# Layer 1 of a two-layer graph network: logits as eight 64-column products, and another order of ScalarE's work at a group's end

## The chip, the cores and the metric

The kernel runs on one core of a Trainium2 chip. Such a core has TensorE (PE in the profile; PEld are its weight loads), VectorE (DVE), ScalarE (ACT), GpSimd (POOL) and SyncE (SP, which here only starts DMAs). They run side by side and wait for one another through semaphores. TensorE writes its products into PSUM, eight banks of 512 f32 columns on 128 partitions[...]. The metric is the device time of one execution in microseconds (us).

## The reference

Two layers work on x (4096 x 512) and a weighted adjacency matrix adj (4096 x 4096). Layer 0 is a dense attention with adj added to its logits. The change is in layer 1, a graph attention with 8 heads of 64 columns:

```python
nX = (x @ W).reshape(n, NHEAD, OUT_DIM).transpose(1, 0, 2)      # then each head's rows are standardized
at1 = jnp.einsum('kno,ok->kn', nX, a1)[:, :, None]
at2 = jnp.einsum('kno,ok->kn', nX, a2)[:, :, None]
kg = jax.nn.leaky_relu(at1 + at2.transpose(0, 2, 1), negative_slope=LK_ALPHA)
kg = kg * graph[None, :, :]
mg = jnp.where(mask[None, :, :], kg, NEG_FILL)
attention = jax.nn.softmax(mg, axis=-1)
y = attention @ nX + nX
...
return jax.nn.elu(y)
```

graph and mask are adj and its nonzero places. So for each head there is a 4096 x 4096 matrix of logits, each the leaky relu of a sum of two numbers, times the edge's weight, with absent edges pushed far down; then an exponential, and a product with the head's values.

## The kernel before, in words

Layer 0 takes a little over the first half of the span and is not touched. Layer 1 then runs 512 steps (STEPS in `fast_path`): 8 chunks of 512 targets (ic) x 2 groups of 4 heads (hg) x 32 blocks of 128 sources (jt). One step handles 128 sources x 512 targets for 4 heads: sources lie on the partitions, targets along the 512 columns. The 32 steps of one (ic, hg) are a group; its results gather in `accs`, a PSUM tile of two banks.

The order of the work is written out by hand: `seq` keeps each engine's instructions in the order of the program text, and the framework puts the semaphores in. The loop at the end of `fast_path` issues for step n:

- `sums(n)`, on TensorE. `z_product` (L1065) makes the sum of the two numbers of each head as a product with only 6 rows to sum over: bf16 pieces of the one number against ones, and ones against pieces of the other. Head number hh sits on partitions 32 hh to 32 hh + 5, so that the four heads use different rows of TensorE's array and run side by side. Two heads (hh 1 and 3) start in the banks r0 and r1; the other two (hh 0 and 2) are added onto what already stands in the tile `l` (two banks). Then eight products with 64 x 64 parts of an identity (L1095) add the masks, in two waves of four that run side by side.
- `left_sums(n + 1)` (L1075), on TensorE: four products of 64 rows and 64 columns, the first part of the next step's `l`; ScalarE turns it by `left_relu` (L1081). The relu has to be done before the next step's `z_product` of hh 0 and 2.
- `right_leaky(n)` (L1113), on VectorE, from r0 and r1 into the SBUF tile `t` (six buffers); `right_weigh(n)` (L1119) on GpSimd multiplies by the edges' weights; `left_weigh(n)` (L1122) on VectorE does that for the heads in `l`.
- `values(n - 4, 0)` and `values(n - 4, 1)` (L1134), on TensorE: f32 products of 64 columns, two heads side by side, added in `accs`.
- `exponent(n - 2)` (L1126), on ScalarE, over all of `t`.

`l` has two buffers and r0 and r1 one each.

At a group's end (step n in which n - 4 was the group's last block) `finish` empties `accs`: ScalarE copies one bank (L1187) and VectorE the other (L1188). Over the next four steps, in the "mid" place between the two halves of the values, `to_rows` (L1198) turns a quarter back to rows on TensorE and `divide` (L1210, L1211) divides it on VectorE; GpSimd's DMAs, an exponential (L1237) and the store follow some steps later. In the kernel before, ScalarE's exponential of step n - 2 is done in two halves there, heads 0 and 1 ahead of its copy and heads 2 and 3 after it. For the 15 groups before the last this is so; at the last group's end no exponential is left to do.

Of the kernel before, what the change touches and what calls it, by code (L numbers as in the profile page):

```python
# [18 lines left out]
P = 128  # L19
# [3 lines left out]
HD = 64  # L23
# [56 lines left out]
def fast_path(  # L80
# [18 lines left out]
    nc = tc.nc  # L99
    seq = tc.keep_in_program_order  # L100
# [155 lines left out]
    def two_halves(t):  # L256
        return t.rearrange("p (g c) -> p g c", g=2)
# [68 lines left out]
    with tc.tile_pool(name="rows_in", bufs=2) as rows_in, tc.tile_pool(  # L326
# [70 lines left out]
        with tc.tile_pool(name="proj_v", bufs=1) as pv, tc.tile_pool(  # L397
# [209 lines left out]
            for k in range(KC):  # L607
                pa = psum.tile([P, 512], F32, name="pa", tag="XZ"[k % 2], bufs=2)
                for c in range(SB):
                    seq(nc.tensor.matmul(  # L610
                        pa, turned["q"][:, c, ts(k, P)], turned["k"][:, c, :],
                        start=c == 0, stop=c == SB - 1,
# [42 lines left out]
            for sb in range(NS):  # L655
                if sb + 2 < NS:
                    xts[sb + 2] = load_x(sb + 2)
                if sb == 1:
                    for k in range(KC):
                        seq(nc.sync.dma_start(  # L660
                            out=w1_sb[:, k, :, 0 : D // 2], in_=two_halves(w1[ts(k, P), :])
# [22 lines left out]
        with tc.tile_pool(name="turns", bufs=6) as turns, tc.tile_pool(  # L684
# [238 lines left out]
            for s in range(0, n_tiles, 2):  # L923
                ic, jt = TILES[s]
# [63 lines left out]
    with tc.tile_pool(name="ga_g", bufs=2) as adjs, tc.tile_pool(  # L988
# [5 lines left out]
        JB = 4  # L994
# [3 lines left out]
        loads, logits, groups = {}, {}, {}  # L998
# [7 lines left out]
        def load_adj(q):  # L1006
            ic, _, jt = STEPS[q * JB]
            z2 = inputs.tile([P, JB * P], BF16, name="z2", tag="z2", bufs=2)
            seq(nc.sync.dma_start(
                out=z2, in_=z2_d[:, STEPS[q * JB][1], jt * P : (jt + JB) * P]  # L1010
            ))
            ng = inputs.tile([P, JB, GC], BF16, name="nb", tag="nb", bufs=2)
            seq(nc.sync.dma_start(
                out=ng, in_=nT_d[jt : jt + JB, :, ts(ic, GC)].rearrange("t p i -> p t i")
            ))

            nx = inputs.tile([P, JB, GC], BF16, name="nx", tag="nx", bufs=2)
            for r in range(2):
                seq(nc.sync.dma_start(
                    out=nx[ts(r, HD)],  # L1020
                    in_=nT_d[jt : jt + JB, ts(1 - r, HD), ts(ic, GC)].rearrange("t p i -> p t i"),
                ))
            g = adjs.tile([P, JB, GC], F32, name="g", tag="g", bufs=2)
            seq(nc.sync.dma_start(
                out=g, in_=gT_d[jt : jt + JB, :, ts(ic, GC)].rearrange("t p i -> p t i")
            ))
            loads[q] = (g, (ng, nx), z2)
# [5 lines left out]
        def open_group(n, queue):  # L1033

            ic, hg, _ = STEPS[n]
            z1_left = z1_lefts[(2 * ic + hg) % 2]
            for first in (0, HD):
                rows = slice(first, first + 6)
                seq(queue.dma_start(out=z1_left[rows, :], in_=z1_d[rows, hg, ts(ic, GC)]))
            z1 = inputs.tile([P, GC], BF16, name="z1", tag="z1", bufs=2)  # L1040
            seq(queue.dma_start(out=z1, in_=z1_d[:, hg, ts(ic, GC)]))
            u4 = inputs.tile([P, 2, GC], F32, name="u4", tag="u4", bufs=2)
            groups[ic, hg] = {"z1": z1, "z1_left": z1_left, "u4": u4}
            load_u4(n, 0, queue)

        def load_u4(n, e, queue):
            ic, hg, _ = STEPS[n]
            seq(queue.dma_start(
                out=groups[ic, hg]["u4"][:, e, :].rearrange("p (b i) -> p b i", i=P),
                in_=u4_d[ic * SB : (ic + 1) * SB, hg * HG + 1 + 2 * e, :]  # L1050
                .unsqueeze(0).to_broadcast([P, SB, P]),
            ))
# [8 lines left out]
        def z_product(n, hh, out, start):  # L1061

            ic, hg, jt = STEPS[n]
            rows = slice(32 * hh, 32 * hh + 6)
            seq(nc.tensor.matmul(  # L1065
                out, loads[n // JB][2][rows, ts(jt % JB, P)], groups[ic, hg]["z1"][rows, :],
                start=bool(start), stop=False, skip_group_check=not start,
            ))

        def left_sums(n):  # L1070

            lefts[n] = psum.tile([P, 2, GC], F32, name="l", tag="l", bufs=2)
            ic, hg, jt = STEPS[n]
            for r, c in ((0, 0), (1, 1), (0, 1), (1, 0)):
                seq(nc.tensor.matmul(  # L1075
                    lefts[n][ts(c, HD), r, :], loads[n // JB][2][ts(r, HD), jt % JB * P + c * HD :][:, :HD],
                    groups[ic, hg]["z1_left"][ts(r, HD), :], start=True, stop=True,
                ))
# [4 lines left out]
        def sums(n):  # L1083

            jt = STEPS[n][2]
            left = lefts[n]
            right = [psum.tile([P, GC], F32, name=f"r{e}", tag=f"r{e}", bufs=1) for e in range(2)]
            out = [left[:, 0, :], right[0], left[:, 1, :], right[1]]
            for hh in (1, 3, 0, 2):
                z_product(n, hh, out[hh], hh % 2)  # L1090
            masks = loads[n // JB][1]
            for first in (1, 0):
                for r, c in ((0, 0), (1, 1), (0, 1), (1, 0)):
                    rows = ts(r, HD)
                    seq(nc.tensor.matmul(  # L1095
                        out[first + 2 * r][ts(c, HD), :], ident_b[rows, rows],
                        masks[r != c][rows, jt % JB, :], start=False, stop=True,
                        skip_group_check=first == 0,
                    ))
            rights[n] = right  # L1100
# [23 lines left out]
        def exponent(n, heads=slice(0, HG)):  # L1124
            t = logits[n][:, heads, :]
            seq(nc.scalar.activation(t, t, AF.Exp))  # L1126
# [28 lines left out]
        def check_early():  # L1155
            ends = work.tile([P, 3], F32, name="ends0", tag="ends0", bufs=1)
            seq(nc.vector.tensor_reduce(ends[:, 0:1], low0, AX.X, ALU.min))
            seq(nc.vector.tensor_reduce(ends[:, 1:2], high0, AX.X, ALU.max))
            seq(nc.vector.tensor_scalar(good[:, 0:1], ends[:, 0:1], TINY, None, ALU.is_ge))
            seq(nc.vector.tensor_scalar(good[:, 1:2], ends[:, 1:2], HUGE0, None, ALU.is_le))  # L1160
            seq(nc.vector.tensor_scalar_mul(ends[:, 2:3], ends[:, 0:1], SPREAD))
            seq(nc.vector.tensor_tensor(good[:, 2:3], ends[:, 1:2], ends[:, 2:3], ALU.is_le))
            check_inverses(3, of_all[:, : of_all.shape[1] - of_last])
# [372 lines left out]
        for n in range(n_steps + 4):  # L1536

            q = n // JB + 1
            if n == n_steps:

                check_early()
                last_in.append(work.tile([P, HG, GC], F32, name="t", tag="t", bufs=6))
                for k, ap in enumerate((own_d[NI - 1, :, :, 1], x1_d[NI - 1, 1])):
                    seq(nc.sync.dma_start(
                        out=last_in[0][:, 2 * k : 2 * k + 2, :].rearrange("p f c -> p (f c)")
                        .rearrange("p (b d) -> p b d", b=SB),
                        in_=ap.rearrange("p b f d -> p b (f d)"),
                    ))
            if n % JB == 0 and q < n_steps // JB:
                load_adj(q)  # L1550
            if n + 10 < n_steps and STEPS[n + 10][2] == 0:
                open_group(n + 10, nc.sync)
            if n + 6 < n_steps and STEPS[n + 6][2] == 0:
                load_u4(n + 6, 1, nc.sync)
            if n < n_steps:
                sums(n)
            for f in left.pop(n, []):
                f()
            if n + 1 < n_steps:
                left_sums(n + 1)  # L1560
            if n < n_steps:
                right_leaky(n)
                right_weigh(n)
            if n + 1 < n_steps:
                left_relu(n + 1)
            done, ready = 0 <= n - 4 < n_steps, 0 <= n - 2 < n_steps
            if done and n < n_steps + 1:
                values(n - 4, 0)
            extra(n, "mid")
            if n < n_steps:  # L1570
                left_weigh(n)
            if done:
                if n < n_steps + 1:
                    values(n - 4, 1)
                if n % JB == 3:
                    loads.pop((n - 4) // JB)
            if n == n_steps + 3:
                for m, hf in ((n - 6, 0), (n - 5, 0), (n - 6, 1), (n - 5, 1)):
                    values(m, hf)
                for hf in range(2):  # L1580
                    values(n - 4, hf)
            if done and STEPS[n - 4][2] == NB - 1:
                if ready:
                    exponent(n - 2, slice(0, 2))
                finish(n, *STEPS[n - 4][:2])
                if ready:
                    exponent(n - 2, slice(2, 4))
            elif ready:
                exponent(n - 2)
            extra(n, "end")  # L1590
# [404 lines left out]
```

## Time and profile before

| | |
|---|---|
| median of 3 runs | 3541.22 us (3538.57 to 3542.74) |
| the profiled execution | 3538.39 us |
| its span, first to last instruction | 3536.6 us |
| granted TensorE clock | 0.996 |
| step 0's first logits product (L1065) | 1935.3 us into the span |
| a usual step of layer 1 | 2.967 us |
| values (L1134) | 4096 matmuls, 605 ns each in the records |
| logits (L1065) | 2048 matmuls, 386 ns |
| masks (L1095) | 4096 matmuls, 402 ns into r, 378 ns into l |
| left sums (L1075) | 2048 matmuls, 380 ns |

The span is what the profile shows from the first instruction to the last; about 1.8 us of the execution lie around it. A matmul's length in a record is modelled, and products on different parts of the array overlap, so that the lengths don't add up to time: what counts is when the next kind of product starts. In a row of the profile the line, the engine and the operation come first, then what is written and read by the program's names, the shape (`6*128` is 6 rows and 128 columns of weights), the count, the busy time in us and after it the mean of one in ns, and last the idle time before it with what ended it.

### The profile page before, as it was taken

The page shows a single profiled execution, that of the slowest core. Times are in us where ns is not written, and L with a number is a line of the kernel's source. Part 1 is how long each engine was busy: PE and PEld are TensorE (multiplying, and loading weights), DVE is VectorE, ACT ScalarE, POOL GpSimd, SP SyncE. Part 2 cuts the span into 40 slices and gives each one's busy share as a digit, 9 for nine tenths or more (in the row PEclk, how much of TensorE's full clock was granted, in tenths as well). Part 3 has the DMA queues.
Part 4 walks back from the last instruction along what each step waited for, and adds up shares of the span by engine and source line. Part 5 has one row for each costly group of instructions (what it writes and reads, how often), then busy time and mean ns, then how long its engine had stood idle before and what let it go on. Part 6 is the DMA issues. An engine that isn't in the chain of part 4 may idle for free.

```text
span 3536.6 us, 59808 instructions
## 1 busy us (share of the span) xinstructions
PE 3492.0 (99%) x21898; PEld 2149.6 (61%) x21898; DVE 2574.3 (73%) x4262; ACT 1771.1 (50%) x1580; POOL 2285.6 (65%) x1863
## 2 busy tenths in 40 slices
PE   9999999999999999999999999999999999999998
PEld 7888888888888888888887223223222323232232
DVE  6765665656565666656567888888888888888887
ACT  2100111111111111111133999999999999999997
POOL 6754444444444444444567888788888888888886
PEclk9999999999999999999999999999999999999999
DMA  6688888888888888888768777787778877777885
GB/s 226 219 247 246 233 232 250 234 244 247 235 246 247 231 252 241 237 248 232 235 135 183 210 207 204 205 208 214 211 209 219 214 215 206 198 209 209 214 213 147
DMA packets 633550, 779.07 MB, mean 220 GB/s; under 512 B 78560, under 2 KB 461216, under 8 KB 624032
## 3 DMA queue, kind: packets, MB, share of 16 engines
q1 hardware_dynamic: 615680, 742.34, 73.5%
q0 software_dynamic: 16464, 31.98, 5.3%
q8 instruction: 174, 2.85, 0.3%
q10 hardware_dynamic: 1104, 0.85, 0.1%
q14 instruction: 128, 1.05, 0.1%
HBM read 592.97 MB, written 174.19 MB: 217 GB/s over the span
## 4 chain that ended last, share of the span: by engine, by line
PE 90%; DVE 7%; ACT 1%; DMA 1%; issue 1%; SPq 0%; DVEq 0%; ACTq 0%
PE accs L1134 25%; PE XZ L722 21%; PE M L777 20%; PE r L1095 4%; PE r L1065 4%; PE l L1075 3%; PE X L508 3%; PE l L1095 3%; PE Z L508 2%; DVE t L1122 2%; PE y L1327 1%; PE pt L1198 1%; DVE x L837 1%; DVE y L1211 1%; PE accs L1327 1%
## 5 line engine op out<-in xcount | busy, mean ns | idle before, releaser
L1119 POOL TENSOR_TENSOR t<-t,g 128x1024 f32<-128x1024 f32 x512 | 1225.6, 2406 | 268.9 <-DVE t L1113 233.3
L1134 PE MATMUL accs<-t,nX 128*64 128x512 f32 x4096 | 1003.0, 605 | 4.6 <-DVE ob L1188 4.6
L1126 ACT ACTIVATE t<-t 128x2048 f32<-128x2048 f32 (+1 forms) x527 | 976.5, 1853 | 0.2 <-POOL t L1119 0.2
L1113 DVE SCALAR_TENSOR_TENSOR t<-u,at2m,r 128x512 f32<-128x512 f32 x1024 | 719.3, 744 | 194.2 <-issue 152.0
L738 ACT ACTIVATE aT<-aT 128x512 f32<-128x512 f32 x256 | 161.2, 630 | 1387.3 <-DVE aT L734 1387.3
L734 DVE TENSOR_TENSOR aT<-aT,XZ 128x256 f32<-128x256 f32 x884 | 348.7, 418 | 575.1 <-PE XZ L722 570.8
L1122 DVE TENSOR_TENSOR t<-l,g 128x1024 f32<-128x1024 f32 x512 | 623.4, 1218 | 0.0
L1081 ACT ACTIVATE l<-l 128x1024 f32<-128x1024 f32 x512 | 516.3, 1008 | 117.5 <-PE l L1075 66.2
L1134 PEld LDWEIGHTS accs<-t,nX 128*64 128x64 f32 x4096 | 246.5, 136 | 461.9 <-issue 449.5
L722 PE MATMUL XZ<-qt,hS 128*128 128x256 f32 x2024 | 479.1, 379 | 1.0
L750 POOL TENSOR_TENSOR S<-aT 128x256 f32<-128x256 f32 x128 | 93.5, 731 | 506.9 <-ACT aT L738 506.9
L722 PEld LDWEIGHTS XZ<-qt,hS 128*128 128x128 f32 x2024 | 383.9, 190 | 55.9 <-DVE aT L734 4.0
L722 PE MATMUL XZ<-qt,hT 128*128 128x256 f32 x1520 | 369.5, 379 | 0.0
L762 POOL TENSOR_TENSOR total<-total,aT 128x256 f32<-128x256 f32 x360 | 323.0, 910 | 9.4
L722 PEld LDWEIGHTS XZ<-qt,hT 128*128 128x128 f32 x1520 | 288.8, 190 | 39.3
L1065 PEld LDWEIGHTS <-z 6*128 6x128 bf16 x2048 | 52.4, 91 | 422.2 <-DVE t L1113 353.8
L751 POOL TENSOR_TENSOR aT<-aT 128x256 f32<-128x256 f32 x128 | 93.6, 731 | 284.1 <-ACT aT L738 284.0
L777 PE MATMUL M<-tv,aT 128*128 128x256 f32 x1024 | 262.6, 379 | 0.0
L777 PE MATMUL M<-v,aT 128*128 128x256 f32 x1024 | 262.6, 379 | 0.0
L777 PE MATMUL M<-v,S 128*128 128x256 f32 x1024 | 242.5, 380 | 0.0
L714 DVE SCALAR_TENSOR_TENSOR gs<-ng,aT 128x512 f32<-128x512 bf16 x252 | 222.7, 884 | 8.7
L777 PEld LDWEIGHTS M<-v,aT 128*128 128x128 f32 x1024 | 194.6, 190 | 26.5
(267 smaller groups left out, 4552.4 us busy)
## 6 DMA issues: line engine op xcount, KB each, us to landing
g<-gT_d SPq DMA_DIRECT2D x128, 1024.0 KB
ag<-in_adj_dram SPq DMA_DIRECT2D x256, 256.0 KB
hS<-s_d SPq DMA_DIRECT2D x64, 1024.0 KB
gT_d<-gs SPq DMA_DIRECT2D x256, 256.0 KB
nb<-nT_d SPq DMA_DIRECT2D x128, 512.0 KB
nx<-nT_d SPq DMA_DIRECT2D x256, 256.0 KB
hT<-h_d SPq DMA_DIRECT2D x64, 768.0 KB
tv<-vt_d SPq DMA_DIRECT2D x128, 384.0 KB
```

Of the source, the lines that this page charges most:

```text
L714: seq(nc.vector.scalar_tensor_tensor(gs, ng, G_MASKED / NEG_BIG, aT, ALU.mult, ALU.add))
L722: seq(nc.tensor.matmul(out, a, b, start=start and k == 0, stop=k == 1, skip_group_check=not start,))
L734: seq(nc.vector.tensor_add(p, before, part))
L762: seq(nc.gpsimd.tensor_add(t, t, a))
L777: seq(nc.tensor.matmul(sums[ic][i][:, u, :], a[:, ts(u, P)], b, start=jt == 0 and u == 0, stop=jt == NB - 2, skip_group_check=u == 1,))
L1081: seq(nc.scalar.activation(lefts[n], lefts[n], AF.Relu, scale=4.0))
L1095: seq(nc.tensor.matmul(out[first + 2 * r][ts(c, HD), :], ident_b[rows, rows], masks[r != c][rows, jt % JB, :], start=False, stop=True, ski ...
L1113: seq(nc.vector.scalar_tensor_tensor(t[:, 2 + e, :], u4[:, e, :], at2m[:, jt, h : h + 1], right[e], ALU.max, ALU.add))
L1119: seq(nc.gpsimd.tensor_mul(t[:, 2:4, :], t[:, 2:4, :], both_heads(n)))
L1122: seq(nc.vector.tensor_mul(logits[n][:, 0:2, :], lefts.pop(n), both_heads(n)))
L1126: seq(nc.scalar.activation(t, t, AF.Exp))
L1134: seq(nc.tensor.matmul(accs[ts(e, HD), hf, :], nX[jt // SB][:, jt % SB, hg * HG + 2 * hf + e, :], t[:, hf + 2 * e, :], start=jt == 0, stop ...
```

## The change

Two edits. In `z_product` each head's product of 128 weight columns is written as two of 64 columns, one after the other: each writes 64 of the 128 partitions of the same bank, from the same 512 columns of `z1`. A step's four matmuls and four weight loads become eight and eight. In the loop, at a group's end, the exponential of step n - 2 isn't halved any more: it is issued whole after `finish`, so that ScalarE's copy of the accumulator comes first.

```diff
@@ -1062,10 +1062,12 @@
 
             ic, hg, jt = STEPS[n]
             rows = slice(32 * hh, 32 * hh + 6)
-            seq(nc.tensor.matmul(
-                out, loads[n // JB][2][rows, ts(jt % JB, P)], groups[ic, hg]["z1"][rows, :],
-                start=bool(start), stop=False, skip_group_check=not start,
-            ))
+            for c in range(2):
+                seq(nc.tensor.matmul(
+                    out[ts(c, HD), :], loads[n // JB][2][rows, jt % JB * P + c * HD :][:, :HD],
+                    groups[ic, hg]["z1"][rows, :],
+                    start=bool(start), stop=False, skip_group_check=not start,
+                ))
 
         def left_sums(n):
 
@@ -1580,11 +1582,9 @@
                 for hf in range(2):
                     values(n - 4, hf)
             if done and STEPS[n - 4][2] == NB - 1:
-                if ready:
-                    exponent(n - 2, slice(0, 2))
                 finish(n, *STEPS[n - 4][:2])
                 if ready:
-                    exponent(n - 2, slice(2, 4))
+                    exponent(n - 2)
             elif ready:
                 exponent(n - 2)
             extra(n, "end")
```

## The prediction

> **What bounds the kernel now.** I read the page first. TensorE (PE) is busy almost all the time; of a pipelined engine that alone proves nothing.
>
> ```profile
> PE   3492.0 (99%) x21898; PEld 2149.6 (61%) x21898; DVE 2574.3 (73%) x4262; ACT 1771.1 (50%) x1580; POOL 2285.6 (65%) x1863
> ```
>
> So I went to the second half of the span, layer 1, and listed one step's weight loads in order of time; they mark where each kind of product begins. Columns: start in us, length, engine, line, operation, form, count.
>
> ```profile
> 2500.40 0.10 PEld L1065 LDWEIGHTS <-z 6*128 6x128 bf16 x4 [0.81 <-DVE t L1113]
> 2500.72 0.14 PEld L1095 LDWEIGHTS <-ident_b 64*64 64x64 bf16 x8 [0.23 <-issue]
> 2500.97 0.12 PEld L1075 LDWEIGHTS <-z 64*64 64x64 bf16 x4
> 2501.50 0.20 PEld L1134 LDWEIGHTS accs<-t,nX 128*64 128x64 f32 x4 [0.41 <-issue]
> 2501.98 0.14 PEld L1134 LDWEIGHTS accs<-t,nX 128*64 128x64 f32 x2 [0.28 <-issue]
> 2502.41 0.14 PEld L1134 LDWEIGHTS accs<-t,nX 128*64 128x64 f32 x2 [0.29 <-issue]
> 2503.36 0.10 PEld L1065 LDWEIGHTS <-z 6*128 6x128 bf16 x4 [0.81 <-DVE t L1113]
> ```
>
> A step is 2503.36 - 2500.40 = 2.967 us (unrounded records), and nearly all steps between group ends repeat it to a nanosecond. Single matmul records, first to first: logits (L1065) to masks 0.325; first mask wave to second 0.240; second to left sums (L1075) 0.216; left sums to values (L1134) 0.316; inside the values 0.480, 0.429, 0.429; last values to the next logits 0.525. These are one chain of PE work without a wait: the "DVE t L1113" of the loads is not the cause, since the same 0.52 from values to the next kind of product is seen at the rare products of L1432 and L1447. The others have room: ScalarE's (ACT's) two activations start 0.92 and about 1.80 apart when back to back, 2.72 in all; the page's rows give VectorE (DVE) 2 x 0.744 + 1.218 = 2.71 and GpSimd (POOL) 2.41. PE sets the step, so a nanosecond on it in a step counts once per step.
>
> What makes 0.325 out of four concurrent streams? The groups of one stretch by form (mean ns after the comma) tell:
>
> ```profile
> L1095 PE MATMUL r<-nb,ident_b 64*64 64x512 bf16 x60 | 12.1, 400 | 0.0
> L1095 PE MATMUL l<-nb,ident_b 64*64 64x512 bf16 x60 | 11.4, 376 | 0.0
> L1065 PE MATMUL l<-z,z 6*128 6x512 bf16 x58 | 11.3, 385 | 0.0
> L1095 PEld LDWEIGHTS <-ident_b 64*64 64x64 bf16 x236 | 4.3, 104 | 6.6 <-issue 6.6
> L1065 PEld LDWEIGHTS <-z 6*128 6x128 bf16 x116 | 2.9, 90 | 23.5 <-DVE t L1113 19.5 <-issue 4.1
> ```
>
> A product whose weights are there already takes 376 ns (modelled length), the first wave after a change of shape 400 with 64-column weights, but 385 with the 128-column logits weights: 24 against 9 ns of visible load. The loads agree: 104 against 90. So 0.325 = 0.216 (a wave) + 0.010 (four products starting 3.4 ns apart) + 0.009 (load) + 0.090 (change of tile shape). Left sums to values: 0.216 + 0.010 + 0.090; values to logits: 0.429 + 0.096.
>
> **What the Trainium skill says.** "TensorEngine Tiling (Array Packing)", Key Properties: a change of tiling mode drains TensorE, and tiles run independently, 32x64 among the modes with eight of them. The trace agrees on the drain: 0.090 to 0.096 at each change, whether rows alone change (left sums to values, 64x64 to 128x64), columns alone (values to L1432, 128x64 to 128x128), or both. The same page, Restrictions: column tiling switches Fast Weight Load off; "TensorE: Matmul & The Clock Gate", Weight-path perf modes, wants 128 weights that are not FP32. That fits 90 against 104 ns. The latter page, Part 3, The mechanism: about 4 ns per further tile (here 3.4), and a weight load overlaps running products only where the row group differs. The trace differs on the last: the third mask load shares its 64 rows with the first product, and is issued 5 ns after that product starts.
>
> **The change part by part.**
> 1. Logits. Four loads of 128 columns and four matmuls become eight of 64. The same 512 columns stream, into the same four banks. Issue: four more pairs x 3.4 ns = 13.6 ns until the last product starts. Load: the first wave waits like the masks', 400 instead of 384.5 ns: 15.5. The changes of shape on both sides stay changes (128x64 to 32x64, 32x64 to 64x64; 0.09 each). Sum 29 ns a step: logits to masks 0.354, a step 2.996. Four pairs x 512 steps = 2048 more loads and as many matmuls on PE's queue; no DMA is added.
>
> The wait on a 3.4 ns start inside a pair on the same rows is not shown for 32-row tiles. Lower bound: no issue cost, 15.5 ns in all, or no load cost, 13.6; a gain only if a drain shrinks (rival below). Upper bound short of a serial pair: the two values products, which share all rows, start 6 to 7 ns apart (they are f32, which may be why). With 7 in each pair the last starts at 4 x 7 + 3 x 3.4 = 38 instead of 10: 28 + 15.5 = 43.5 ns. I take 29, since the masks show 3.4 with shared rows.
>
> 2. Where it is hidden. At each of the 15 inner group ends five steps have a PE wait after the logits that another chain sets. In the first PE waits for the accumulator copies (0.38 beyond its own work before L1134); in the next four, left sums wait 0.30 for VectorE, which divides first (periods 3.737, against 2.967). A delay of 0.029 disappears in each: 75 steps. About five of the first steps also wait on other engines. 512 - 75 - 5 = 432 steps pay; were all to pay, it would be 2.3 us more.
> 432 x 0.029 = 12.5 us.
>
> 3. ScalarE at the group's end. Its instructions around one, in order:
>
> ```profile
> 2835.54 1.01 ACT L1081 ACTIVATE l<-l 128x1024 f32<-128x1024 f32 x1
> 2836.46 1.05 ACT L1126 ACTIVATE t<-t 128x1024 f32<-128x1024 f32 x1
> 2837.40 0.58 ACT L1187 COPY ob<-accs 128x512 f32<-128x512 f32 x1
> 2837.88 1.06 ACT L1126 ACTIVATE t<-t 128x1024 f32<-128x1024 f32 x1
> 2838.84 1.02 ACT L1081 ACTIVATE l<-l 128x1024 f32<-128x1024 f32 x1
> 2839.78 1.90 ACT L1126 ACTIVATE t<-t 128x2048 f32<-128x2048 f32 x1
> 2842.62 1.01 ACT L1081 ACTIVATE l<-l 128x1024 f32<-128x1024 f32 x1 [0.94 <-PE l L1075]
> ```
>
> It looks as if the half exponential held the copy back. It doesn't: in all 15 cases the copy starts 0.642 to 0.644 after the last values matmul of both halves starts, while its distance to the half exponential's end varies (0.100 to 0.107 overlap). The half just fills a wait. Who waits for the copy:
>
> ```profile
> 2838.02 0.69 DVE L1188 COPY ob<-accs 128x512 f32<-128x512 f32 x1 [0.29 <-ACT ob L1187]
> ```
>
> VectorE's copy follows ScalarE's by 0.03, and PE's next values follow that. The list of waits has PE idle for it by 0.3 at a time:
>
> ```profile
> PE accs L1134 <- DVE ob L1188: 4.6, 15, 0.3
> ```
>
> Moved ahead, ScalarE's copy stands at 2837.40 still, ScalarE idles about 0.85 in front of it, and queued behind it are the undivided exponential (2837.88 to 2839.79; two halves of 1.05 and 1.06 become one of 1.90, 0.21 less) and the next relu of the left sums, from 2839.69 to 2840.70 instead of 2838.84 to 2839.86. That relu is late next: PE's logits add onto it from 2841.09, so 0.39 of slack, some 0.3 after a semaphore. The exponential itself is wanted a step after that. ScalarE then makes up the rest in its 0.94 idle before 2842.62. Cost 0; gone cover would cost the excess over 0.3, once in 15 groups. No DMA and no queue is crossed.
>
> Sum on the profiled execution: 3536.6 of span + 1.8 around it = 3538.4, + 12.5 = 3550.9. The median of the runs, 3541.22, is 2.8 above that execution; so I predict 3541.2 + 12.5 = 3553.7. A measurement of this kernel tells about 0.2%, 7.1 us, from no change.
>
> **Rivals.**
> - One term only (load hidden behind the longer issue, or issue behind the load): 432 x 0.0136 to 0.0155 = 5.9 to 6.7 us, 3547 to 3548. For: the two overlap in time. Against: the last product needs its own load.
> - Pairs 7 ns apart: 432 x 0.0435 = 18.8, 3560. For: the values' spacing. Against: the masks'.
> - Pairs on the same rows run one after the other: another wave, 0.216 + 0.016 a step, still under the 0.30 that hides it at group ends: 432 x 0.232 = 100 us, 3641. Against: masks share rows and run together.
> - The other side, faster: with all products now 64 columns wide, PE no longer drains before and after the logits. It takes 2 x 0.093 away for 0.029: 432 x 0.157 = 68 us, 3473; ScalarE's 2.72 is not reached. It decides as soon as the two drains shrink by more than 0.029 together. For: only rows would change at both borders. Against: left sums to values changes rows alone and pays 0.090.
> - The copy waits in truth for its own half of the accumulator and is freed by the new order: PE's 0.38 x 15 = 5.7 us go, less 0.4 for steps that then pay: 3541.2 + 12.5 - 5.3 = 3548. Against: the constant 0.643 after both halves, and PE's first half waiting for VectorE's copy of the second.
>
> **How the numbers follow.** Chances: 29 ns 0.60 (3553.7), pairs at 7 ns 0.12, one term 0.10, copy freed 0.05, serial pairs 0.05, no drain 0.08. Range 3546 to 3561: the first four, 0.87, with the medians' own spread of some 2 us. Slower by over 0.2%: 0.60 + 0.12 + 0.05 + half of the copy's = 0.79; within: 0.10 + the other half = 0.13; faster 0.08.
>
> **What would show it.** Right: logits records near 400 ns, loads near 104, eight starts over some 24 ns; logits to masks 0.354; steps of 2.996; the five long steps at 3.74 to 3.79 unchanged; ScalarE idle before its copy by 0.85, PE's wait for the copies still 0.3 x 15. Wrong: a step under 2.967, logits to masks over 0.5, a copy that starts before both value halves end, or PE waiting for the relu in the step after.

## The result, and the profile after

The changed kernel takes 3549.44 us (median of 12 runs, 3548.02 to 3552.23) against 3539.85 us for the kernel before (12 runs): 9.6 us more, a ratio of 1.0028 with a 95% interval of 1.0019 to 1.0037. So it is slower, by about as little as can be told from no change. Medians are of the fast executions; two that took over 8000 us, one of the kernel before and one of the sixteen products below, are left out. The span of the profiled execution is 3547.3 us, 10.7 more than before.

The page of the changed kernel shows the 2048 further products (23946 instead of 21898), ScalarE's 15 fewer instructions, and the engines' busy times about as they were:

```profile
PE 3504.5 (99%) x23946; PEld 2161.6 (61%) x23946; DVE 2573.4 (73%) x4262; ACT 1772.0 (50%) x1565; POOL 2285.3 (64%) x1863
```

One usual step's weight loads in order of time, changed kernel (start us, length us, engine, line, operation, form, count):

```profile
2498.18 0.12 PEld L1066 LDWEIGHTS <-z 6*64 6x64 bf16 x8 [0.81 <-DVE t L1115]
2498.54 0.14 PEld L1097 LDWEIGHTS <-ident_b 64*64 64x64 bf16 x8 [0.23 <-issue]
2498.78 0.12 PEld L1077 LDWEIGHTS <-z 64*64 64x64 bf16 x4
2499.31 0.20 PEld L1136 LDWEIGHTS accs<-t,nX 128*64 128x64 f32 x4 [0.41 <-issue]
...
2501.18 0.13 PEld L1066 LDWEIGHTS <-z 6*64 6x64 bf16 x8 [0.81 <-DVE t L1115]
```

A step is 2.991 us now (the median of all steps, unrounded records), 24 ns longer. It is the logits that have grown: from their first product to the first mask 0.352 us instead of 0.325, and from their last product to the first mask 0.328 instead of 0.315. All the other stretches of the step stay as they were, but for the last: from the last values to the next logits 0.522 to 0.523 instead of 0.525. The groups of one stretch by form (busy us, mean ns after the comma) point to two reasons:

```profile
L1066 PE MATMUL l<-z,z 6*64 6x512 bf16 x116 | 11.8, 398 | 0.0
L1097 PE MATMUL r<-nb,ident_b 64*64 64x512 bf16 x58 | 11.7, 400 | 0.0
...
L1066 PEld LDWEIGHTS <-z 6*64 6x64 bf16 x232 | 3.6, 101 | 23.5 <-DVE t L1115 19.5 <-issue 4.1
```

A logits product is 398 ns long in the record, not 385, as the first masks are 400. That length is modelled, but the distance from the last logits product to the first mask, taken from starts alone, grew by the same 13 ns. I read it as a wait for the weights. And the eight products start over 0.023 us, where four started over 0.010: another 13 ns.

At the group's end, ScalarE's instructions in order:

```profile
2841.53 1.01 ACT L1083 ACTIVATE l<-l 128x1024 f32<-128x1024 f32 x1 [0.17 <-PE l L1077]
2843.40 0.58 ACT L1189 COPY ob<-accs 128x512 f32<-128x512 f32 x1 [0.85 <-PE accs L1136]
2843.88 1.92 ACT L1128 ACTIVATE t<-t 128x2048 f32<-128x2048 f32 x1
2845.69 1.02 ACT L1083 ACTIVATE l<-l 128x1024 f32<-128x1024 f32 x1
```

Where half an exponential stood, ScalarE waits 0.85 us for PE's values (L1136). The copy still starts 0.64 after the last values matmul starts. The relu that follows (L1083) ends at 2846.71, and PE adds onto its output from 2847.08: 0.37 of room, and 0.37 to 0.38 at all 15 inner group ends. PE's list of waits:

```profile
PE accs L1136 <- DVE ob L1190: 4.3, 15, 0.3
```

PE's wait for VectorE's copy is 0.3 less in total than the 4.6 of before: the longer logits in front of it use up part of this wait.

### The profile page after: what moved, and what is told of

Read it like the earlier page. It is cut to its first block, busy times and chain, and to the rows that moved or that the text cites. A ratio compares the mean times of both kernels' runs of the same rounds, so it can differ in the third digit from the quotient of the medians.

```text
span 3547.3 us, 63904 instructions
## 1 busy us (share of the span) xinstructions
PE 3504.5 (99%) x23946; PEld 2161.6 (61%) x23946; DVE 2573.4 (73%) x4262; ACT 1772.0 (50%) x1565; POOL 2285.3 (64%) x1863
## 4 chain that ended last, share of the span: by engine, by line
PE 91%; DVE 7%; DMA 1%; issue 1%; ACT 0%; SPq 0%; DVEq 0%; ACTq 0%
PE accs L1136 26%; PE XZ L722 21%; PE M L777 20%; PE r L1097 4%; PE r L1066 4%; PE l L1077 3%; PE X L508 3%; PE l L1097 3%; PE Z L508 2%; DVE t L1124 2%; PE y L1329 1%; PE pt L1200 1%; DVE x L837 1%; DVE y L1213 1%; PE accs L1329 1%
## 5 line engine op out<-in xcount | busy, mean ns | idle before, releaser
L1136 PE MATMUL accs<-t,nX 128*64 128x512 f32 x4096 | 1003.2, 605 | 4.3 <-DVE ob L1190 4.3
L1128 ACT ACTIVATE t<-t 128x2048 f32<-128x2048 f32 x512 | 973.5, 1902 | 0.2 <-POOL t L1121 0.2
L1083 ACT ACTIVATE l<-l 128x1024 f32<-128x1024 f32 x512 | 516.3, 1008 | 114.4 <-PE l L1077 113.0
L1136 PEld LDWEIGHTS accs<-t,nX 128*64 128x64 f32 x4096 | 246.6, 136 | 461.5 <-issue 449.2
L1066 PEld LDWEIGHTS <-z 6*64 6x64 bf16 x4096 | 64.4, 101 | 422.1 <-DVE t L1115 353.8
L1066 PE MATMUL r<-z,z 6*64 6x512 bf16 x2048 | 209.8, 400 | 6.3 <-DVE t L1115 5.6
```

The lines of the kernel that those rows point to most:

```text
L1066: seq(nc.tensor.matmul(out[ts(c, HD), :], loads[n // JB][2][rows, jt % JB * P + c * HD :][:, :HD], groups[ic, hg]["z1"][rows, :], start=bo ...
L1083: seq(nc.scalar.activation(lefts[n], lefts[n], AF.Relu, scale=4.0))
L1136: seq(nc.tensor.matmul(accs[ts(e, HD), hf, :], nX[jt // SB][:, jt % SB, hg * HG + 2 * hf + e, :], t[:, hf + 2 * e, :], start=jt == 0, stop ...
```

## The experiments

All are edits of the kernel before, compared with runs of it on the same chip (median 3539.02 us for the products alone, the order alone, the sixteen products and the two tiles with the halved exponential; 3538.51 for the other three). What was expected is quoted as it was put down before the run. The tile shape of a product is the rows and columns of TensorE's array that it uses; PE drains when it lets what runs come to its end before it starts the next product.

**The products alone.** The first half of the change, with the exponential still halved around the copy.

```diff
+            for c in range(2):
+                seq(nc.tensor.matmul(
+                    out[ts(c, HD), :], loads[n // JB][2][rows, jt % JB * P + c * HD :][:, :HD],
...
```

> Only the logits in eight products of 64 columns; the exponential stays halved around the copy. If the products are the whole cost: logits to masks 0.352 us and a step of 2.991 as in the changed kernel, +10 us or a ratio of 1.0028 to the kernel before, and the five long steps at a group's end unchanged. If the order of ScalarE's work has a share, this run stands more than 2 us away from the changed kernel's +9.6.

Measured: 3548.49 us, ratio 1.0025 (1.0016 to 1.0035); logits to masks 0.352, a step of 2.991, the five long steps as before (3.79, three of 3.73 to 3.74, and 3.29). The loads of one of its steps:

```profile
2498.77 0.13 PEld L1066 LDWEIGHTS <-z 6*64 6x64 bf16 x8 [0.81 <-DVE t L1115]
2499.12 0.14 PEld L1097 LDWEIGHTS <-ident_b 64*64 64x64 bf16 x8 [0.23 <-issue]
```

That is +9.5 us against the whole change's +9.6: the products are the cost.

**The order alone.** The second half of the change.

```diff
-                if ready:
-                    exponent(n - 2, slice(0, 2))
                 finish(n, *STEPS[n - 4][:2])
                 if ready:
-                    exponent(n - 2, slice(2, 4))
+                    exponent(n - 2)
```

> Only the undivided exponential after ScalarE's copy; the logits stay four products of 128 columns. My account: ratio 1.000 within 0.001; the copy still starts 0.64 us after the last values matmul, ScalarE sits idle 0.85 before it, and PE still waits about 0.3 for VectorE's copy, 15 times. Rival, the copy is freed by the new order: 5 us faster and PE's wait for the copies gone. Rival, the relu behind the exponential comes too late: PE waits before the logits two steps after each group's last values, up to 0.5 us, 15 times: up to 8 us slower.

Measured: 3539.46 us, ratio 1.0002 (0.9994 to 1.0010). ScalarE at the group's end and PE's wait for the copies, from this run's timeline and list of waits:

```profile
2837.01 0.58 ACT L1187 COPY ob<-accs 128x512 f32<-128x512 f32 x1 [0.85 <-PE accs L1134]
2837.49 1.92 ACT L1126 ACTIVATE t<-t 128x2048 f32<-128x2048 f32 x1
```

```profile
PE accs L1134 <- DVE ob L1188: 4.7, 15, 0.3
```

The copy is not freed (0.85 idle ahead of it, PE's wait unchanged), and the later relu, with 0.37 of room at each group end, holds nobody up. Both rivals about the order fall: they asked for 5 us less or up to 8 us more. The copy starts 0.638 to 0.639 after the last values matmul here and 0.642 to 0.644 in the kernel before, so the half exponential held it by some 4 ns.

**Four products of 64 columns, the issue taken away.** Only the first 64 of the 128 columns are multiplied, and in r0 and r1 the masks of the others start their bank. Half of the sources lack their logits product, so this is a time and not a layer.

```diff
-            seq(nc.tensor.matmul(
-                out, loads[n // JB][2][rows, ts(jt % JB, P)], groups[ic, hg]["z1"][rows, :],
+            for c in range(1):
+                seq(nc.tensor.matmul(
+                    out[ts(c, HD), :], loads[n // JB][2][rows, jt % JB * P + c * HD :][:, :HD],
...
-                        masks[r != c][rows, jt % JB, :], start=False, stop=True,
+                        masks[r != c][rows, jt % JB, :], start=first == 1 and c == 1, stop=True,
```

> Only the first 64 of each head's 128 weight columns: four products of 64 columns instead of eight, so half of the sources lack the logits product, which is left out (their masks start the bank instead). It takes the issue of four pairs away and leaves the load of 64 columns. Two terms: logits to masks 0.352 - 0.0136 = 0.338, a step of 2.977, 432 x 0.010 = +4 us. If the issue alone made the cost: 0.325 and no difference. If the load alone made it: 0.352 and +10 us.

Measured: logits to masks 0.338, a step of 2.978, 3542.75 us, +4.2 us, ratio 1.0012 (1.0006 to 1.0019). A group by form and the loads of one step of this run:

```profile
L1066 PE MATMUL r<-z,z 6*64 6x512 bf16 x58 | 11.6, 398 | 0.0
```

```profile
2496.53 0.11 PEld L1066 LDWEIGHTS <-z 6*64 6x64 bf16 x4 [0.81 <-DVE t L1115]
2496.87 0.14 PEld L1097 LDWEIGHTS <-ident_b 64*64 64x64 bf16 x8 [0.23 <-issue]
```

The records are 398 ns long, the four start over 0.010, and from the last of them to the first mask it is 0.328, as in the changed kernel. So going from 128 to 64 columns alone costs 13 ns, and the four further pairs of a load and a product the other 14.

**Sixteen products of 32 columns, the issue raised.** The same sums with four quarters to a head.

```diff
+            for c in range(4):
+                seq(nc.tensor.matmul(
+                    out[ts(c, R), :], loads[n // JB][2][rows, jt % JB * P + c * R :][:, :R],
...
```

> The logits as sixteen products of 32 columns, the same sums. Two terms (3.4 ns for each further pair, and a first load that is seen in proportion to its columns): twelve pairs more than four cost 41 ns, while the load of 32 columns is about half of the 24 ns that are seen with 64, so about the 9 of before; logits to masks 0.365, a step near 3.005, 432 x 0.038 = +16 us, ratio 1.0046. If the load alone counted, the logits would be back at 0.325 and the time at that of before. If the products ran in several waves, logits to masks would be over 0.5.

Measured: logits to masks 0.364, a step of 3.003, 3553.09 us in the five executions that count, +14.1 us, ratio 1.0039 (1.0026 to 1.0052). The groups of this run by form:

```profile
L1066 PE MATMUL r<-z,z 6*32 6x512 bf16 x232 | 11.8, 384 | 0.0
...
L1066 PEld LDWEIGHTS <-z 6*32 6x32 bf16 x464 | 4.0, 87 | 23.5 <-DVE t L1115 19.5 <-issue 4.1
```

The product is back at 384 ns (87 for the load), and the last logits product is followed by the first mask after 0.314, so the load term is gone again, while the sixteen start over 0.050 us: 3.3 ns for each pair, also where four in a row use the same array rows. The two terms are seen apart, the issue in this run, the load in the run before.

**Two widths in one step.** Heads 1 and 3 keep one product of 128 columns, heads 0 and 2 get two of 64.

```diff
+            if hh % 2:
+                seq(nc.tensor.matmul(
+                    out, loads[n // JB][2][rows, ts(jt % JB, P)], groups[ic, hg]["z1"][rows, :],
...
+                return
+            for c in range(2):
...
```

> Heads 1 and 3 as one product of 128 columns each, heads 0 and 2 as two of 64: within the logits the columns alone change (32x128 to 32x64). If every change of shape drains: 0.216 + 0.003 + 0.009 + 0.090 for the first two, then 0.216 + 0.010 + 0.024 + 0.090, so logits to masks 0.658, a step of 3.297, 432 x 0.33 + 75 x 0.03 = +145 us, about 3685. If a change of columns alone does not drain, the six run as one wave: 0.34 to 0.35 and under +10 us.

Measured: logits to masks 0.656, a step of 3.298, 3683.78 us, +145.3 us, ratio 1.0411 (1.0396 to 1.0427). The loads of one step of this run:

```profile
2549.16 0.09 PEld L1066 LDWEIGHTS <-z 6*128 6x128 bf16 x2 [0.81 <-DVE t L1121]
2549.48 0.11 PEld L1072 LDWEIGHTS <-z 6*64 6x64 bf16 x4 [0.23 <-issue]
2549.82 0.14 PEld L1103 LDWEIGHTS <-ident_b 64*64 64x64 bf16 x8 [0.23 <-issue]
```

The two halves of the logits no longer run together: the 64-column loads come 0.32 us after the 128-column ones, though their array rows are free. A change of columns alone drains PE as any other change does. The 0.33 that a step grows is more than a drain: the products of the second width also stream after those of the first, where all of one width run side by side. The rival by which PE would stop draining once all products were 64 columns wide also falls with the changed kernel itself: where only rows change, from values (128x64) to logits (32x64), 0.522 of the 0.525 us remains.

**Two accumulator tiles.** What holds the copies at a group's end? The accumulator as two PSUM tiles of one bank each for the steps (layer 1's projections keep the one of two banks, in a pool that is closed ahead of the first values).

```diff
+            if n == 3:
+                wide.__exit__(None, None, None)
...
+                accs += [halves.tile([P, GC], F32, name=f"accs{k}", tag=f"accs{k}", bufs=1) for k in range(2)]
...
-                    accs[ts(e, HD), hf, :], nX[jt // SB][:, jt % SB, hg * HG + 2 * hf + e, :],
+                    accs[hf][ts(e, HD), :], nX[jt // SB][:, jt % SB, hg * HG + 2 * hf + e, :],
...
-                seq(nc.scalar.copy(ob[0], accs[:, 0, :]))
-                seq(nc.vector.tensor_copy(ob[1], accs[:, 1, :]))
+                seq(nc.scalar.copy(ob[0], accs[0]))
+                seq(nc.vector.tensor_copy(ob[1], accs[1]))
```

> The kernel before with the accumulator as two PSUM tiles of one bank for the steps, in place of one of two banks. If the copies wait for both halves, and for each other, only because they belong to one tile: VectorE's copy no longer follows ScalarE's, PE's 0.3 of idle before the values is gone and the first of the five long steps falls from 3.79 to 3.41; 0.38 x 15 = 5.7 us faster, ratio 0.9984. If the order of the copies has another cause (the engines' own order), nothing changes.

Measured: 3532.45 us, 6.6 us under the kernel before, ratio 0.9982 (0.9975 to 0.9989). VectorE's instructions at a group's end of this run, in order, and ScalarE's copy:

```profile
2834.18 1.22 DVE L1124 TENSOR_TENSOR t<-l,g 128x1024 f32<-128x1024 f32 x1
2835.32 0.68 DVE L1190 COPY ob<-accs 128x512 f32<-128x512 f32 x1
```

```profile
2835.08 0.58 ACT L1189 COPY ob<-accs 128x512 f32<-128x512 f32 x1
```

VectorE's copy follows its own work without a gap, and starts 0.34 us before ScalarE's copy of the other bank has ended. PE's wait for the copies no longer appears in its list of waits; the first long step is 3.41 instead of 3.79, which is 5.7 us over 15 group ends, and what follows the last step's logits is 0.8 us shorter. The semaphores in the two traces show why, at all 15 group ends: with one tile, the only signal from TensorE's values comes after the last product of both halves, and VectorE's copy waits for a signal of ScalarE's copy. With two tiles TensorE signals after each half, and VectorE's copy waits for TensorE and its own engine, not for ScalarE. The two copies read different banks in both kernels, so it is the shared tile that put them in a row.

**Two accumulator tiles, and the copy ahead of an undivided exponential.**

> The two accumulator tiles together with the undivided exponential after ScalarE's copy. If the single tile is what held the copies, ScalarE's copy now starts when its own half is there, right behind the relu at about 0.25 us before the last values matmul ends its issue, PE's 0.3 of idle is gone, and the time is that of the two tiles with the halved exponential, since PE had no further wait there: about 5.7 us under the kernel before. If the order matters after all, it differs from that run by more than 2 us.

Measured: 3531.86 us, ratio 0.9981 (0.9975 to 0.9988). Against the kernel before on its own chip that is 6.7 us less, not to be told from the 6.6 with the halved exponential. ScalarE at the group's end of this run, and the values' products:

```profile
2832.43 1.01 ACT L1083 ACTIVATE l<-l 128x1024 f32<-128x1024 f32 x1
2833.47 0.58 ACT L1189 COPY ob<-accs 128x512 f32<-128x512 f32 x1
2833.95 1.92 ACT L1128 ACTIVATE t<-t 128x2048 f32<-128x2048 f32 x1
```

```profile
2832.31 1.94 PE L1136 MATMUL accs<-t,nX 128*64 128x512 f32 x8
```

Now the copy is right behind the relu, and starts 0.19 before the last values matmul of the other half does: it doesn't wait for that half. The order that the change chose does what it looks like only here, and even here it saves no time, since nobody waits for ScalarE's copy by then.

This run says something of the one before it, too. There, with the same two tiles, the copy starts 0.642 to 0.644 after the last values matmul in all 15 cases, exactly as in the kernel before, though it need not wait for that matmul: what stands ahead of it on its own engine is the half exponential.

## Why the prediction was right

**The sign and the place** held: PE's chain sets the step, and 0.024 us more in a step showed in full outside the places that hide it. 432 paying steps x 0.024 = 10.4 us, against 10.7 in the span and 9.6 between the medians. The predicted 3553.7 lies 4.3 above the result: 2.9 of it are the size of the cost (12.5 predicted, 9.6 measured), 1.4 the median of before, which stood at 3541.22 with 3 runs and at 3539.85 with 12.

**What the time alone would not have told.** The result lies nearer to the rival of one term only (3547 to 3548) than to the predicted 3553.7; with the later median of before under both, it lies about midway. And the range of 3546 to 3561 took in four accounts. That both terms are there is shown by the starts in the trace and by the runs with four and sixteen products, not by the total.

**The size: 29 ns predicted, 24 measured.** The issue term was 13.6 and measured 13 (0.023 less 0.010). The load term was 15.5, taken from the masks' 400 ns; the logits' records came to 398, so 13.5. The third term was held at nothing, "The changes of shape on both sides stay changes": the one from values to logits became 2 to 3 ns shorter. The four kernels whose logits begin with products of under 128 columns in that place (the whole change, the products alone, the four and the sixteen) have 0.522 to 0.523, the others 0.525. It is not that the columns stop changing there: in the run with sixteen they go from 64 to 32, and it has 0.523 as well. So it goes with the width of the first load; why is open.

**The cover** held. The five long steps at a group's end stay at 3.79, 3.74 (three times) and 3.29 us; the prediction gave 3.74 to 3.79 for all five, but the fifth was 3.29 before, too. Inside them the left sums' wait went from 0.303 to 0.278 and the wait ahead of the values from 0.38 to 0.36, which is the 0.025 that disappears there.

**The order of ScalarE's work** cost nothing, as forecast: 0.85 idle ahead of the copy, the copy at 0.64 after the last values, the relu 0.37 ahead of its use (0.39 predicted), and 1.0002 when tried alone. The prediction wanted some 0.09 of that room for a semaphore without a figure; the one hand-over between engines that its lines show, from ScalarE's copy to VectorE's, takes 0.03.

The reason that it gave was weaker than it looked, and here it had luck. It took the constant 0.643 after the last values as the proof that the half exponential didn't hold the copy. But the half exponential kept nearly as constant a distance (0.100 to 0.107 of overlap), it let the copy go only some 4 ns after the values did, and the two-tile run has the same 0.643 where the copy need not wait for the last values. What settles it is the run of the order alone, which took the half exponential away: the copy came 4 ns sooner, and no more.

**The rivals.** One term only: the four-product and the sixteen-product runs show both terms. Pairs 7 ns apart, and serial pairs: the starts are 3.3 ns apart. No drain: the two-width run. The copy freed by the order: it needs two tiles first.

**The drain and the loads.** Of what the prediction took from the Trainium skill, the drain ("TensorEngine Tiling (Array Packing)", Key Properties; the 32x64 mode with its eight tiles stands under Available Configurations) carried it: the two-width run shows it where only columns change, and the eight products of the changed kernel do run side by side. The one that the trace of before had contradicted, weight loads overlapping only in other row groups ("TensorE: Matmul & The Clock Gate", Part 3, The mechanism), is contradicted by the sixteen products too, four of which follow one another on the same rows at 3.3 ns. That 64 columns lose a fast load fits the traces: a load of 128 columns reads its weights in four pieces of 32 columns there, those of 64 and 32 in one. From 32 to 64 columns the visible part grows by 14 ns, so at that rate 128 would show some 50, an estimate from these two; 9 are seen. But no run switches the fast load off at one width, so this part stays a reading.

## What to carry to other kernels

Where TensorE sets the step and small products run side by side, cutting them finer bought nothing here, as they ran together already: it added 3.3 ns for each further product, and 64 columns lost the shorter wait of 128 for the first weights after a change of tile shape. Count the changes of shape in a step first: here each costs some 0.09 us, and one more in the middle of the logits, which also parted products that had run side by side, cost the kernel 4%.

An idle engine ahead of a copy, or a half operation that just fills that time, doesn't tell what the copy waits for. Neither does a constant distance to a candidate: in a loop where the engines keep step, several stand at one. Take a candidate away, or split what they share, and see whether the copy moves. And look at what one tile holds: here ScalarE's copy waited for products of a bank that it doesn't read, and VectorE's for ScalarE's, only because both banks were one tile.

## What was not expected of the hardware

- The visible part of a weight load after a change of shape is not in proportion over all widths: about 9 ns with 128 bf16 columns, 22 to 24 with 64, 8 with 32. A logits product of 32 columns is as cheap to begin as one of 128.
- Rows that are free are no help against a change of width: 0.32 us pass between the 128-column and the 64-column loads of the two-width run, as much as from the left sums to the values.
